# A routing softmax by silu in place of powers, with its planner's haste and logits changed, in a fused state-space and mixture-of-experts kernel

## The chip, the cores and the metric

The kernel runs on one core of a Trainium2 chip. A core has five engines that run side by side, each with its own queue in order: TensorE (PE, matrix products and transposes into PSUM), VectorE (DVE), ScalarE (ACT, activation functions from a loaded table), GpSimd (POOL), and SyncE (SP), which here only issues DMA transfers. They wait for one another through semaphores. The metric is the time of the program on the device in microseconds (us), the median of three runs.

## The reference

The input `x` is 16 sequences (blocks) of 512 positions with 128 features. Two layers follow one another, each with a residual: a linear state-space layer, then a layer of 8 experts of which all are computed and mixed by weights.

```python
x = x + layernorm(ssm(layernorm(x)))        # B_w, C_w, 64 rotating states, D
x = x + layernorm(ffn(layernorm(x)))

def ffn(x):                                  # E = 8 experts, F = 512
    router_probs = softmax(x @ w_router)             # 8 per position
    gate_weights = softmax(x @ w_gating / 0.1)       # 8 per position
    g = einsum("bsh,ehf->ebsf", x, w_gate)
    u = einsum("bsh,ehf->ebsf", x, w_up)
    expert_out = einsum("ebsf,efh->ebsh", silu(g) * u, w_down)
    cw = router_probs * gate_weights
    cw = cw / (sum(cw) + 1e-9)
    return einsum("ebsh,bse->bsh", expert_out, cw)
```

The part that the change touches is the routing: the two softmaxes and `cw`, 16 exponentials per position.

## The kernel before

**Work and slots.** A block is 512 positions. Its expert work is cut into 32 slots: 8 experts with 4 pieces of 128 hidden units. In slot n the kernel issues on TensorE the gate product `g` (`up`, three matmuls of 128x512), the up product `uu` (three), and, four slots late (`LAG`), the down product `d` of an earlier slot (`down`, three). Three matmuls stand for one product because every operand is split into a high part and a low rest (`mm3`, lines 354 to 357: high x high, low x high, high x low). ACT turns `g` into `sg` by silu (L601), DVE multiplies `sg` and `uu` (`gate`, L612), ACT makes the high part `hi` (L617), and the low rest `lo` (L623) is made on POOL or on DVE: `lo_pool[n]` picks POOL when the planner's sum for POOL is below that for DVE. If it is POOL, the product goes to an SBUF tile `hh`; otherwise it stays in the PSUM bank of `uu`, which is free only when DVE has made `lo`. There are two banks for `g`, three for `uu`, two for `d`, and a single one, tag "f", for all else.

**The planner.** The other work is written as generators: `front(b)` (the state-space layer of block b and the normalised input `xh`, `xl` of its experts), `route(b)` (the routing), `back(b)` (the last normalisation and the output). Each `yield` names how many slots later at the earliest the next step may come, its costs in us on DVE, ACT and POOL, and "f" where it takes the shared PSUM bank. `steps` (L834) goes through the open generators in each slot and issues a step if the planner's sums (`take`, a slot of 1.94 us) leave room for it. So the order on each engine's queue is fixed when the program is built. `begin` opens the chain of block b 67 slots before its experts (`LEAD`), block 1 at slot 0, block 2 at slot 4. A chain with `hurry` gets two steps a slot and loses one slot of each wait; block 1 has it, and blocks 2 and 3 get it 16 slots ahead of their experts. Steps of a hurried chain that take the bank are issued ahead of the slot's `g`.

**The routing.** The logits are 16 numbers a position. Blocks 0 to 2 get them from four full-precision matmuls of 16 columns (`lg`, L436); later blocks (`wide`, L264) from two matmuls of 512 columns (`lp`, L443 and L444) with four copies of the split router weights `wr4`, which DVE transposes in four pieces (`lt`, L450). DVE takes the maximum (L456) and subtracts it (L457). The exponentials: in block 0 two ACT instructions with `Exp` (L462, L463); in all other blocks eight POOL instructions that raise the constants e and e^10 (`bases`) to the power of the logits (L467). DVE then sums, inverts and scales (L470 to L472), multiplies the two softmaxes (L476), sums, adds 1e-9, inverts (L478 to L480), writes the result into a padded tile (`cwp`, L483) and transposes it (`cwT`, L485). Four DMAs on SP's queue write it to DRAM and further ones read it back, spread over all partitions (`cwb`, L502), for `combine`, which weighs each expert's output.

**The start.** Up to the first slot the state-space layer of block 0 runs by itself with all engines on one chain: rotation tables on DVE, `u` (normalised input, ACT L552), its transposes and `bu` on TensorE, a scan on DVE, `yp` on TensorE. ACT's queue begins with two DMA issues, the copies of bT and cT (L283, L284), two diagonals (L693, L694) and `u`. SP's queue issues the loads in the order in which the code names them; the router and gating weights (`wrg`, L136 and L137) come behind the first three expert weights. The first splits of expert weights are partly made on TensorE (`rest`), partly on POOL (`wgl`, `wul`, `wdl`, L117).

Of the kernel before, what the change touches and what calls it, by code (L numbers as in the profile page):

```python
# [2 lines left out]

# [8 lines left out]
F32 = mybir.dt.float32  # L12
F32R = mybir.dt.float32r
AF = mybir.ActivationFunctionType
ALU = mybir.AluOpType
# [8 lines left out]
N = 64  # L24
# [5 lines left out]
OWN = 8  # L30
WARM = 4
AHEAD = 3
FILL = 8
LN_EPS = 1e-5


# [12 lines left out]
def sandwich(ctx, tc, x, a_params, B_w, C_w, Dv, w_router, w_gating, w_gate, w_up, w_down, sines, out):  # L49
# [71 lines left out]
    small_ins = work("small_ins")  # L121
    st = small_ins[: N // 2, :P]
    nc.sync.dma_start(out=st, in_=sines)
    av = const.tile([N // 2, 1], F32, name="av")
    act.dma_start(out=av, in_=a_params.unsqueeze(1))
    load_x(0)
    bw = small_ins[:N, P : 2 * P]
# [7 lines left out]
    wrg = const.tile([D, 2, E], F32, name="wrg")  # L135
    nc.sync.dma_start(out=wrg[:, 0], in_=w_router)  # L136
    nc.sync.dma_start(out=wrg[:, 1], in_=w_gating)  # L137
    dbc = const.tile([P, D], F32, name="dbc")
    for k in range(AHEAD, OWN):
        load_w(k)  # L140
# [5 lines left out]
    make_identity(nc, ident)  # L146
    neghalf = const.tile([P, NT], F32, name="neghalf")
    gp.memset(neghalf, -0.5)
    zero = const.tile([P, 1], F32, name="zero")
    gp.memset(zero, 0.0)  # L150
    bases = const.tile([P, NT, 2, E], F32, name="bases")
    gp.memset(bases[:, :, 0], math.e)
    gp.memset(bases[:, :, 1], math.exp(10.0))
    cwp = []
    for i in range(2):
        t = const.tile([P, NT, 32], F32, name=f"cwp{i}")
# [105 lines left out]


    def wide(b):  # L264
        return b > 2

    bT = [const.tile([D, P], F32R, name=f"bT{i}") for i in range(2)]
    cT = const.tile([P, D], F32, name="cT")
# [1 line left out]
    bT32 = const.tile([D, P], F32, name="bT32", tag="first")  # L270

    wr4 = []

    const.tile([P, FILL], F32, name="fill")

    def transposed_weights():
        pb = bank(ps_u, "u", "pb")[:, :N]
# [76 lines left out]
    def mm3(ps, w, cs, mh, ml, first, last):  # L354
        pe.matmul(ps, w[0][:, cs], mh, start=first, stop=False)  # L355
        pe.matmul(ps, w[1][:, cs], mh, start=False, stop=False)  # L356
        pe.matmul(ps, w[0][:, cs], ml, start=False, stop=last)  # L357
# [67 lines left out]
    def route(b):  # L425

        G2 = NT * 2
        yield 1, 0, 0, 0, "f"
        bc = lambda t, n: t.unsqueeze(2).broadcast_to([P, n, E])
        ez = small.tile([P, G2, E], F32, name="ez", bufs=2)  # L430
        mx = small.tile([P, G2], F32, name="mx", bufs=2)
        if not wide(b):
            lg = ps_f.tile([P, G2, E], F32, name=f"lg{b}", tag="f")
            xT = blocks[b]["xT"]
            for c in range(NT):
                pe.matmul(  # L436
                    lg[:, 2 * c : 2 * c + 2], xT[:, P * c : P * c + P], wrg.rearrange("d g e -> d (g e)"),
                    start=True, stop=True,
                )
            yield 1, 0.4, 0, 0  # L440
        else:
            lp = ps_f.tile([P, T], F32, name=f"lp{b}", tag="f")
# [8 lines left out]
            own[0] = False  # L451
            yield 1, 0.7, 0, 0
            l4 = lt.rearrange("p j (i k) -> p j i k", i=2)
            vec.tensor_tensor(ez.rearrange("p (c g) e -> p c (g e)", g=2), l4[:, :, 0], l4[:, :, 1], ALU.add)
            lg = ez
        vec.tensor_reduce(mx, lg, AX.X, ALU.max)  # L456
        vec.tensor_tensor(ez, lg, bc(mx, G2), ALU.subtract)  # L457
        if not wide(b):
            own[0] = False
        if b == 0:  # L460
            e4 = ez.rearrange("p (c g) e -> p c g e", g=2)
            act.activation(e4[:, :, 0], e4[:, :, 0], AF.Exp)  # L462
            act.activation(e4[:, :, 1], e4[:, :, 1], AF.Exp, scale=10.0)  # L463
        else:
            for i in range(G2):
                yield 1, 0, 0, 1.62
                gp.tensor_tensor(ez[:, i], bases.rearrange("p c g e -> p (c g) e")[:, i], ez[:, i], ALU.pow)  # L467
        yield 2, 0.65, 0, 0
        sm = small.tile([P, G2], F32, name="sm", bufs=2)
        vec.tensor_reduce(sm, ez, AX.X, ALU.add)  # L470
        vec.reciprocal(sm, sm)
        vec.tensor_tensor(ez, ez, bc(sm, G2), ALU.mult)  # L472
        yield 1, 0.75, 0, 0
        pr = ez.rearrange("p (c g) e -> p c g e", g=2)
        cw0 = small.tile([P, NT, E], F32, name="cw0", bufs=2)
        vec.tensor_tensor(cw0, pr[:, :, 0], pr[:, :, 1], ALU.mult)  # L476
        cs = small.tile([P, NT], F32, name="cs", bufs=2)
        vec.tensor_reduce(cs, cw0, AX.X, ALU.add)  # L478
        vec.tensor_scalar(cs, cs, 1e-9, None, ALU.add)
        vec.reciprocal(cs, cs)  # L480
        yield max(1, 32 * b - 8 - now[0]), 0.45, 0, 0
        cwt = cwp[b % 2]
        vec.tensor_tensor(cwt[:, :, 0:E], cw0, bc(cs, NT), ALU.mult)  # L483
# [105 lines left out]
    dps = {}  # L589
    late = []  # L590

    def up(n):
        b, e, fc = n // 32, n // 4 % 8, n % 4
        B = blocks[b]
        cs = slice(128 * fc, 128 * fc + 128)
        g = ps_g.tile([P, T], F32, name=f"g{n}", tag="g")
        mm3(g, W[0, e], cs, B["xh"], B["xl"], True, True)
        u = ps_u.tile([P, T], F32, name=f"uu{n}", tag="u")
        mm3(u, W[1, e], cs, B["xh"], B["xl"], True, True)
        s = hp.tile([P, T], F32, name=f"sg{n}", tag="sg", bufs=2)  # L600
        act.activation(s, g, AF.Silu)  # L601
        pend[n] = s, u
# [49 lines left out]
    def chain(b):  # L652
        yield from front(b)
        yield from route(b)
# [147 lines left out]

    def first():
        nonlocal routed
        for _ in range(2):
            next(first_route)
        routed = next(first_route)

# [25 lines left out]
    def steps(n, ahead=False):  # L834

        for x in list(side):
            hurry = x[3]
            for _ in range(1 + hurry):
                bank = "f" in x[1][3:]
                if ahead != bool(hurry and bank):  # L840
                    break
                if n >= x[0] and not (own[0] and bank) and take(x[1][:3]):
                    own[0] = own[0] or bank
                    y = next(x[2], None)
                    if y is None:
                        side.remove(x)
                        break
                    x[0], x[1] = n + (y[0] if y[4:] else max(y[0] - hurry, 0)), y[1:]

    own[0] = False  # L850
    for n in range(total + LAG):
# [5 lines left out]
        if 0 <= n - 1 < total:  # L857
            take((0, 0, 1.23) if lo_pool[n - 1] else (0.6, 0, 0), (9, 9, 9))
            split_hi(n - 1)
        for step in side:  # L860
            if step[4] in (2, 3) and n == 32 * step[4] - 16:
                step[3] = 1
        if n < total:
            steps(n, True)
            if n == 0:
                first()
            up(n)
        if n == 0:
# [61 lines left out]
```

## Time and profile before

| | |
|---|---|
| median of 3 runs | 1125.45 us (1125.32 to 1125.46) |
| profiled execution | 1125.5 us, of it 1123.7 between the first and the last instruction |
| TensorE busy | 1105.3 us, 98% |
| DVE, POOL, ACT busy | 882.6, 781.3, 710.8 us |
| first expert matmul | 24.19 us |
| last 6.7 us | TensorE busy 0.54 us |
| powers on POOL | 120 instructions of 1.65 us, 195.9 us |
| table loads on ACT | two of 1.28 us, at 1.77 and 25.33 us |

"busy" is the time in which an engine has an instruction in work. Matmuls overlap, so the duration of one (0.39 us) is longer than the step from one to the next; how much work TensorE gets through is read from starting times. A name such as `L612` is a line of the kernel before. An answer of the timeline has the start and the duration in us, then engine, line, operation, output and inputs, shape and number; in brackets stands how long the engine was idle before it and what ended that. A row of a group ends with busy time, mean duration in ns, and idle time before.

### The profile page before, as it was taken

The numbers are of one execution on the slowest core, as the hardware profiler recorded it, in microseconds if no ns is written. First come the engines' busy times: TensorE is split into PE (matmuls) and PEld (weight loads), VectorE is DVE, ScalarE is ACT, GpSimd is POOL, SyncE is SP. The second block draws the span as 40 slices with busy tenths as digits, with TensorE's granted clock in tenths as the row PEclk, the third lists the DMA queues.
The fourth block names the chain that finished last, engine by engine and source line by source line (L and its number), as shares of the span: only waits on it lengthen the run. The fifth ranks groups of instructions, "written<-read, shape, count | busy, mean of one in ns | idle before, by whom it ended". The sixth has DMA issues, their size and how long they took to land.

```text
span 1123.7 us, 16035 instructions
## 1 busy us (share of the span) xinstructions
PE 1105.3 (98%) x4909; PEld 906.6 (81%) x4909; DVE 882.6 (79%) x2056; ACT 710.8 (63%) x1347; POOL 781.3 (70%) x651
## 2 busy tenths in 40 slices
PE   7999999999999999999999999999999999999997
PEld 5778888878878888888888888888888888888886
DVE  7887777887878888787887878878787887777666
ACT  4775756666565665766666675666766666666563
POOL 2688685786959568685876768668685876848452
PEclk9999999999999999999999999999999999999999
DMA  5240402212131221302203130130312202121020
GB/s 157 74 133 1 123 29 84 68 39 85 38 114 29 58 66 57 94 29 76 76 30 94 38 113 29 57 92 17 110 29 76 76 20 75 29 76 30 29 76 10
DMA packets 66950, 71.22 MB, mean 63 GB/s; under 512 B 7216, under 2 KB 49328, under 8 KB 66864
## 3 DMA queue, kind: packets, MB, share of 16 engines
q1 hardware_dynamic: 66448, 70.04, 20.8%
q8 instruction: 38, 0.62, 0.2%
q14 instruction: 48, 0.39, 0.1%
q10 hardware_dynamic: 416, 0.16, 0.1%
HBM read 54.98 MB, written 15.20 MB: 62 GB/s over the span
## 4 chain that ended last, share of the span: by engine, by line
PE 90%; DVE 4%; POOL 2%; ACT 1%; issue 1%; DMA 0%; DVEq 0%; POOLq 0%; ACTq 0%
PE g L355 10%; PE g L356 10%; PE g L357 10%; PE d L355 10%; PE d L357 10%; PE d L356 10%; PE uu L355 10%; PE uu L356 10%; PE uu L357 10%; PE yp L404 1%; POOL ez L467 1%; ACT sg L601 1%; DVE uu L612 0%; DVE lo L623 0%; DVE hh L612 0%
## 5 line engine op out<-in xcount | busy, mean ns | idle before, releaser
L617 ACT CAST hi<-uu 128x512 fp32r<-128x512 f32 x325 | 191.0, 588 | 219.8 <-DVE uu L612 205.6
L623 POOL TENSOR_TENSOR lo<-hh,hi 128x512 fp32r<-128x512 f32 x187 | 244.8, 1309 | 120.8 <-ACT hi L617 118.2
L601 ACT ACTIVATE sg<-g 128x512 f32<-128x512 f32 x512 | 306.8, 599 | 20.8 <-PE g L357 17.2
L612 DVE TENSOR_TENSOR uu<-sg,uu 128x512 f32<-128x512 f32 x325 | 225.1, 692 | 105.8 <-ACT sg L601 103.1
L623 DVE TENSOR_TENSOR lo<-uu,hi 128x512 fp32r<-128x512 f32 x325 | 223.0, 686 | 102.9 <-ACT hi L617 97.5
L646 POOL TENSOR_TENSOR acc<-acc,ct 128x512 f32<-128x512 f32 x109 | 147.3, 1351 | 94.9 <-DVE ct L643 90.2
L617 ACT CAST hi<-hh 128x512 fp32r<-128x512 f32 x187 | 116.2, 621 | 149.6 <-DVE hh L612 146.0
L355 PE MATMUL g<-xh,wgh 128*128 128x512 f32 x512 | 202.6, 396 | 0.8 <-ACT sg L601 0.4
L355 PE MATMUL uu<-xh,wuh 128*128 128x512 f32 x512 | 199.7, 390 | 2.6 <-DVE lo L623 2.4
L356 PE MATMUL g<-xh,wgl 128*128 128x512 f32 x512 | 199.5, 390 | 0.0
L357 PE MATMUL g<-xl,wgh 128*128 128x512 f32 x512 | 199.5, 390 | 0.0
L356 PE MATMUL uu<-xh,wul 128*128 128x512 f32 x512 | 199.3, 389 | 0.0
L357 PE MATMUL uu<-xl,wuh 128*128 128x512 f32 x512 | 199.3, 389 | 0.0
L355 PE MATMUL d<-hi,wdh 128*128 128x512 f32 x512 | 199.3, 389 | 0.0
L356 PE MATMUL d<-hi,wdl 128*128 128x512 f32 x512 | 199.2, 389 | 0.0
L357 PE MATMUL d<-lo,wdh 128*128 128x512 f32 x512 | 199.2, 389 | 0.0
L467 POOL TENSOR_TENSOR ez<-bases,ez 128x8 f32<-128x8 f32 x120 | 195.9, 1652 | 1.6 <-DVE ez L457 1.6
L612 DVE TENSOR_TENSOR hh<-sg,uu 128x512 f32<-128x512 f32 x187 | 127.1, 680 | 11.0 <-ACT sg L601 9.2
L355 PEld LDWEIGHTS g<-xh,wgh 128*128 128x128 f32 x512 | 96.2, 188 | 24.5 <-ACT sg L601 5.7
L355 PEld LDWEIGHTS uu<-xh,wuh 128*128 128x128 f32 x512 | 96.1, 188 | 24.4 <-DVE lo L623 4.3
L357 PEld LDWEIGHTS g<-xl,wgh 128*128 128x128 f32 x512 | 96.1, 188 | 20.3
L356 PEld LDWEIGHTS uu<-xh,wul 128*128 128x128 f32 x512 | 96.1, 188 | 20.2
(185 smaller groups left out, 1346.8 us busy)
## 6 DMA issues: line engine op xcount, KB each, us to landing
cwb<-scw SPq DMA_DIRECT2D x48, 512.0 KB
cwb<-scw SPq DMA_DIRECT2D x32, 256.0 KB
xt<-in_L_attn_u_dram SPq DMA_DIRECT2D x15, 256.0 KB
sco<-ob SPq DMA_DIRECT2D x60, 64.0 KB
ot<-sco SPq DMA_DIRECT2D x15, 256.0 KB
out_dram<-x SPq DMA_DIRECT2D x15, 256.0 KB
scr_u<-blk_u SPq DMA_DIRECT2D x52, 64.0 KB
ft_u<-scr_u SPq DMA_DIRECT2D x13, 256.0 KB
```

Source lines behind the costliest of these rows:

```text
L355: pe.matmul(ps, w[0][:, cs], mh, start=first, stop=False)
L356: pe.matmul(ps, w[1][:, cs], mh, start=False, stop=False)
L357: pe.matmul(ps, w[0][:, cs], ml, start=False, stop=last)
L404: pe.matmul(yp[:, c], v[:, P * c : P * c + P], cT, start=True, stop=True)
L467: gp.tensor_tensor(ez[:, i], bases.rearrange("p c g e -> p (c g) e")[:, i], ez[:, i], ALU.pow)
L601: act.activation(s, g, AF.Silu)
L612: vec.tensor_tensor(h, s, u, ALU.mult)
L617: act.copy(hi, pend[n])
L623: (gp if lo_pool[n] else vec).tensor_tensor(lo, h, hi.bitcast(F32), ALU.subtract)
L646: add = lambda: eng.tensor_tensor(acc, acc, t, ALU.add)
```

## The change

- The exponentials of all blocks come from ACT's silu. With y = logit - maximum and S = silu(y - 1), S / ((y - 1) - S) equals e^(y - 1), and the constant factor drops out of the softmax. So `route` gets one `Silu` instruction for all 64 columns with a bias of -1, and DVE gets a subtraction of both, a reciprocal of 64 columns and a product.
- The two softmaxes are no longer scaled one by one: `zz` is the product of the unscaled exponentials, one reduction sums the three parts, and the 1e-9 is scaled by the product of two sums.
- The powers and `bases` go, and `Exp` of block 0 goes.
- The factor 10 of the gating logits is put into the weights: ACT scales `wrg[:, 1]` right behind its two DMA issues.
- `wide` holds from block 1 on, and `wr4` is made in slot 16.
- Blocks 2 and 3 get no haste. Block 1's chain starts in slot 4 with haste, block 2's in slot 5. Bank steps of a hurried chain come between `g` and `uu`.
- `av` lies in `small_ins`; the tile `fill` goes.

```diff
-    av = const.tile([N // 2, 1], F32, name="av")
+    av = small_ins[: N // 2, T - 1 : T]
     nc.sync.dma_start(out=wrg[:, 1], in_=w_gating)
+
+    act.activation(wrg[:, 1], wrg[:, 1], AF.Copy, scale=10.0)
...
-    zero = const.tile([P, 1], F32, name="zero")
+    zo = const.tile([P, 2], F32, name="zo")
+    zero, minus1 = zo[:, 0:1], zo[:, 1:2]
     gp.memset(zero, 0.0)
-    bases = const.tile([P, NT, 2, E], F32, name="bases")
-    gp.memset(bases[:, :, 0], math.e)
-    gp.memset(bases[:, :, 1], math.exp(10.0))
+    gp.memset(minus1, -1.0)
...
     def wide(b):
-        return b > 2
+        return b > 0
...
         vec.tensor_reduce(mx, lg, AX.X, ALU.max)
-        vec.tensor_tensor(ez, lg, bc(mx, G2), ALU.subtract)
+        vec.tensor_tensor(y, lg, bc(mx, G2), ALU.subtract)
         if not wide(b):
             own[0] = False
-        if b == 0:
-            e4 = ez.rearrange("p (c g) e -> p c g e", g=2)
-            act.activation(e4[:, :, 0], e4[:, :, 0], AF.Exp)
-            act.activation(e4[:, :, 1], e4[:, :, 1], AF.Exp, scale=10.0)
-        else:
-            for i in range(G2):
-                yield 1, 0, 0, 1.62
-                gp.tensor_tensor(ez[:, i], bases.rearrange("p c g e -> p (c g) e")[:, i], ez[:, i], ALU.pow)
-        yield 2, 0.65, 0, 0
-        sm = small.tile([P, G2], F32, name="sm", bufs=2)
-        vec.tensor_reduce(sm, ez, AX.X, ALU.add)
-        vec.reciprocal(sm, sm)
-        vec.tensor_tensor(ez, ez, bc(sm, G2), ALU.mult)
-        yield 1, 0.75, 0, 0
-        pr = ez.rearrange("p (c g) e -> p c g e", g=2)
-        cw0 = small.tile([P, NT, E], F32, name="cw0", bufs=2)
-        vec.tensor_tensor(cw0, pr[:, :, 0], pr[:, :, 1], ALU.mult)
+        yield 1, 0, 0.25, 0
+        act.activation(ez, y, AF.Silu, bias=minus1)
+
+        own[0] = own[0] and not wide(b)
+        yield 1, 0.7, 0, 0
+        vec.scalar_tensor_tensor(y, y, 1.0, ez, ALU.subtract, ALU.subtract)
+        vec.reciprocal(y, y)
+        vec.tensor_tensor(ez, ez, y, ALU.mult)
+        yield 1, 0.95, 0, 0
+        vec.tensor_tensor(zz, e4[:, :, 0], e4[:, :, 1], ALU.mult)
+
+        sm = small.tile([P, G2 + NT], F32, name="sm", bufs=2)
+        vec.tensor_reduce(sm, zq, AX.X, ALU.add)
+        s2 = sm[:, :G2].rearrange("p (c g) -> p c g", g=2)
         cs = small.tile([P, NT], F32, name="cs", bufs=2)
-        vec.tensor_reduce(cs, cw0, AX.X, ALU.add)
-        vec.tensor_scalar(cs, cs, 1e-9, None, ALU.add)
+        vec.tensor_tensor(cs, s2[:, :, 0], s2[:, :, 1], ALU.mult)
+        vec.scalar_tensor_tensor(cs, cs, 1e-9, sm[:, G2:], ALU.mult, ALU.add)
         vec.reciprocal(cs, cs)
...
-    def up(n):
+    def up(n, between):
         mm3(g, W[0, e], cs, B["xh"], B["xl"], True, True)
+        between()
         u = ps_u.tile([P, T], F32, name=f"uu{n}", tag="u")
...
-        for step in side:
-            if step[4] in (2, 3) and n == 32 * step[4] - 16:
-                step[3] = 1
         if n < total:
-            steps(n, True)
             if n == 0:
                 first()
-            up(n)
+            up(n, lambda: steps(n, True))
         if n == 0:
             begin(n, 0, first_route, 1, routed)
-            if NB > 1:
-                begin(n, 1, chain(1), 1)
...
-        if n == 32:
+        if n == 16:
             w4 = wrg.rearrange("d g e -> d (g e)").unsqueeze(1).broadcast_to([D, 4, 2 * E])
...
         for i in range(NB):
-            if i > 1 and n == max(4, 32 * i - LEAD):
-                begin(n, i, chain(i))
+            if i > 0 and n == max(i + 3, 32 * i - LEAD):
+                begin(n, i, chain(i), i == 1)
```

`first`, which issues block 0's logits and the start of its routing ahead of slot 0, takes one step more, so that the silu is issued there.

More of the change, by code (lines that the diff above doesn't have):

```diff
@@ L1 @@
-import math
 from contextlib import ExitStack
@@ L32 @@
 AHEAD = 3
-FILL = 8
 LN_EPS = 1e-5
@@ L272, in sandwich @@
     wr4 = []
-    const.tile([P, FILL], F32, name="fill")
     def transposed_weights():
@@ L429, in route @@
         bc = lambda t, n: t.unsqueeze(2).broadcast_to([P, n, E])
-        ez = small.tile([P, G2, E], F32, name="ez", bufs=2)
+        y = small.tile([P, G2, E], F32, name="y", bufs=1)
+        zq = small.tile([P, G2 + NT, E], F32, name="zq", bufs=2)
+        ez, zz = zq[:, :G2], zq[:, G2:]
+        e4 = ez.rearrange("p (c g) e -> p c g e", g=2)
         mx = small.tile([P, G2], F32, name="mx", bufs=2)
@@ L450, in route @@
                 vec.transpose(lt[k].rearrange("p j i -> p (j i)"), lp[k, P * q : P * q + P])
-            own[0] = False
             yield 1, 0.7, 0, 0
             l4 = lt.rearrange("p j (i k) -> p j i k", i=2)
-            vec.tensor_tensor(ez.rearrange("p (c g) e -> p c (g e)", g=2), l4[:, :, 0], l4[:, :, 1], ALU.add)
-            lg = ez
+            vec.tensor_tensor(y.rearrange("p (c g) e -> p c (g e)", g=2), l4[:, :, 0], l4[:, :, 1], ALU.add)
+            lg = y
         vec.tensor_reduce(mx, lg, AX.X, ALU.max)
-        vec.tensor_tensor(ez, lg, bc(mx, G2), ALU.subtract)
+        vec.tensor_tensor(y, lg, bc(mx, G2), ALU.subtract)
@@ L482, in route @@
         cwt = cwp[b % 2]
-        vec.tensor_tensor(cwt[:, :, 0:E], cw0, bc(cs, NT), ALU.mult)
+        vec.tensor_tensor(cwt[:, :, 0:E], zz, bc(cs, NT), ALU.mult)
         cwT = small.tile([P, NT, 32], F32, name="cwT", tag="cwT", bufs=2)
@@ L804, in first @@
         nonlocal routed
-        for _ in range(2):
+        for _ in range(3):
             next(first_route)
```

## The prediction

> **What bounds the kernel now.** I read the page first: TensorE against the rest, and the chain that ended last.
>
> ```profile
> span 1123.7 us, 16035 instructions
> ...
> PE 1105.3 (98%) x4909; PEld 906.6 (81%) x4909; DVE 882.6 (79%) x2056; ACT 710.8 (63%) x1347; POOL 781.3 (70%) x651
> ...
> PE 90%; DVE 4%; POOL 2%; ACT 1%; issue 1%; DMA 0%; DVEq 0%; POOLq 0%; ACTq 0%
> ```
>
> TensorE is full. So relief elsewhere counts only where TensorE waits. Where that is, the busy time by stretches tells (columns: stretch, its length, then busy time of each engine):
>
> ```profile
> 24.20:36.40 12.20, 9.58 (x40) 6.33 (x39) 9.46 (x32) 7.67 (x17) 6.68 (x7) 1.00 0.01 2
> 36.40:99.70 63.30, 61.75 (x278) 49.14 (x279) 52.57 (x104) 46.27 (x91) 53.09 (x43) 1.00 0.30 92
> ...
> 205.00:355.00 150.00, 148.46 (x657) 120.90 (x656) 119.75 (x269) 92.94 (x181) 111.65 (x91) 1.00 0.22 65
> 355.00:1000.00 645.00, 645.00 (x2886) 534.71 (x2886) 514.57 (x1172) 417.64 (x785) 466.46 (x380) 1.00 0.20 60
> ```
>
> From 355 to 1000 us TensorE is busy 645.00 of 645.00 us, although the powers sit on POOL there too. Nothing can be won there by emptying POOL. Third, TensorE's timeline:
>
> ```profile
> 5.12 1.86 PE L178 MATMUL hot<-ident 128*128 128x96 f32 x8
> ...
> 12.77 0.58 PE L178 MATMUL hot<-ident 128*128 128x96 f32 x4
> 14.11 0.71 PE L739 MATMUL yp<-cT,spare 128*128 128x128 f32 x4 [0.76 <-DVE spare L738]
> ...
> 16.80 0.38 PE L739 MATMUL yp<-cT,spare 128*128 128x128 f32 x1 [0.26 <-DVE spare L738]
> ...
> 31.56 0.40 PE L357 MATMUL g<-xl,wgh 128*128 128x512 f32 x1
> 33.60 0.50 PE L355 MATMUL uu<-xh,wuh 128*128 128x512 f32 x1 [1.64 <-DVE lo L623]
> ...
> 600.91 0.39 PE L355 MATMUL g<-xh,wgh 128*128 128x512 f32 x1
> ...
> 602.95 0.39 PE L355 MATMUL g<-xh,wgh 128*128 128x512 f32 x1
> ```
>
> A steady slot takes 2.04 us (602.95 - 600.91), nine matmuls at 0.227; slots 0 to 3 have no `d` and need 1.36. In the same timeline a slot with `bu` takes 0.70 more, with two-pass logits `lp` 0.46, with `yp` 0.91 (the next slot's 0.10 included), with four-column logits `lg` 0.95 (0.14 included), with four transposes 0.36. Against these needs the first `g` of slots 0, 5, 32, 64, 96, 128, 160, 192 (24.19, 36.36, 99.72, 168.38, 236.01, 304.21, 373.99, 441.65) leaves as lost: 4.33 in slots 0-4, 3.75 in 5-31, 0.81, 0.27, 0.81, 2.39, 0.27 in blocks 1 to 5; later blocks take 67.39 each with nothing lost. So 12.6 us can be lost at most less, beside the start before 24.19.
>
> What makes the first loss, by the timelines of DVE and POOL:
>
> ```profile
> 30.21 0.91 DVE L472 TENSOR_TENSOR ez<-ez,sm 128x64 f32<-128x64 f32 x1
> 31.15 1.17 DVE L476 TENSOR_TENSOR cw<-ez 128x32 f32<-128x32 f32 x1
> ```
>
> ```profile
> 29.75 1.28 POOL L623 TENSOR_TENSOR lo<-hh,hi 128x512 fp32r<-128x512 f32 x1
> 30.99 1.28 POOL L117 TENSOR_TENSOR wdl<-raw,wdh 128x512 fp32r<-128x512 f32 x1
> ```
>
> These two take 0.23 and 0.18 elsewhere; here each ends when POOL's 128x512 instruction ends (31.03, 32.27). A DVE instruction with both inputs in SBUF waits for such a POOL instruction; against a power on POOL L472 kept its 0.23.
>
> **Part 1: the scaling of the gating weights at the head of ACT's queue.** It waits for `w_gating`.
>
> ```profile
> 5.16 0.43 SPq L137 DMA_DIRECT2D wrg<-in_L_ffn_w_gating_dram  x1
> ```
>
> ```profile
> 4.05 0.27 ACT L283 COPY bT<-pb 128x128 f32<-128x128 f32 x1 [1.00 <-PE pb L278]
> ...
> 6.55 0.49 ACT L552 ACTIVATE u<-xt,nmh,rsh 128x128 f32<-128x128 f32 x1 [0.42 <-DVE nmh L548]
> ```
>
> The semaphore of that load ends at 7.98 in this trace, behind three 256 KB weight loads. Everything behind it on ACT waits: the copies of bT and cT, the two diagonals, then `u` (6.55). At ACT's own pace from 8.05 (0.2, 0.17, 0.17, 0.21, 0.3 from start to start) `u` starts near 9.05: 2.5 late, and with it the transposes, `bu` and `yp` L713. TensorE's waits for DVE ahead of both L739 groups (0.76 and 0.26, some 0.3 more because modelled ends overlap) absorb about 1.3; 1.2 reaches the second L739, the statistics behind it and so the first `g`. Beyond that TensorE now idles some 2.6 us before the transposes, and it starts slow: eight `hot` in 1.86 (0.23 each) at 5, four in 0.58 (0.145) at 12.8. If the pace comes later by up to 3 us of such work, a further 3 x (1 - 0.145/0.23) = 1.1. Bounds: 0 (absorbed) to 2.6; I take +1.8.
>
> [...]
>
> **Part 2: slots 0-4.** Two exponentials (0.23, 0.21) go and one silu comes (128x64; bounds 0.23 for 128x32 and 0.49 for 128x128, I take 0.33). The built instruction order still has two table loads: one ahead of the scaling, one ahead of the first silu. The load (1.28, at 25.33) no longer stands behind DVE's subtraction but directly behind the weight cast that ends at 24.46, so the first `sg` comes 0.6 earlier. Then DVE, counted from the first `g`: `uu` 2.45-3.15; the new subtraction of both meets POOL's `wdl` (three weight parts now run back to back, 0.35 to 4.14) and ends at 4.37; reciprocal of 64 columns (L471 takes 0.204 for 8, L480 0.178 for 4: 0.0065 per column, so 0.57); product 0.23; `lo` to 5.78, `hh` to 6.43; five small ones to 7.43; the last product meets POOL's `lo` (to 8.43), the transpose, `uu` of slot 2 to 9.55, its cast 10.20, `sg` of slot 3 10.73, the `g` of slot 5 at 10.8. Before it stood at 12.17 with 0.36 of transposes that now come in slot 9: **-1.0**. Bounds: +1 if one more product meets POOL, -3 if none does.
>
> **Part 3: slots 5-31.** Block 1's front starts 4 slots later (8 us), so its statistics now meet slots 4-7: the single-input `ve` waits for a weight part as L299 did (1.03 against 0.17), and I count 1.4 lost in slots 7-9. Behind that, the sum of DVE's durations over what TensorE's slots last runs up to 2.0-3.4 us of arrears in slots 12-24, where before 3-4.6 stood; I take 1.5 lost there. 2.9 for 3.75: **-0.8**; bounds -2.5 and +1.5. Block 1's weights `cwT` now stand in slot 32, and the product that needs them in slot 41, 18 us later; the four writes, first reads and landing took 8.3 us (34.61 to 42.9), so SP's queue hides them. `xh` comes in slot 28 for slot 32.
>
> **Part 4: powers and haste gone.**
>
> ```profile
> L467 POOL TENSOR_TENSOR ez<-bases,ez 128x8 f32<-128x8 f32 x120 | 195.9, 1652 | 1.6 <-DVE ez L457 1.6
> ```
>
> POOL loses 196 us; by the built order its `lo` go from 187 to 239 (52 x 1.31 = +68), DVE's from 325 to 273 (-36 us). DVE's routing grows by some 0.5 us a block (reciprocal 0.57; `sm`, `cs` reductions and small ones about even), ACT's by 0.33, under its slack. The new wait: DVE's subtraction waits for the silu, which stands on ACT behind `sg` and two norms (2 x 0.39); DVE idles some 0.4, and the gate queued behind it needs the next `sg` anyway. Arrears in blocks 3-12 reach 1.7 us, before 3.1. The 3.47 lost in blocks 3-5 (among them `bu` waiting for the logits' transposes at 336, now three slots apart) should go to 0.5: **-3.0**, bounds -3.5 and 0. Blocks 1-2: about equal (1.08 to 1.0, **-0.1**).
>
> **Part 5: logits in two passes** for blocks 1 and 2, on TensorE itself: 2 x (0.95 - 0.46) = **-1.0**. The tail does not change; `av` inside `small_ins`, the constants, and bank steps of block 1 between `g` and `uu` issue the same instructions, nothing.
>
> Sum: +1.8 - 1.0 - 0.8 - 3.0 - 0.1 - 1.0 = -4.1 on the profiled 1125.5 (span 1123.7 and 1.8 around it; the median 1125.45 is the same): **1121.4 us**.
>
> **Rivals.**
> A, the forecast: own range 1118.5 to 1124.
> B, slower: POOL's freed time goes into 128x512 instructions, and DVE's six new two-input instructions in each block meet them. For: the 1.17 above; 52 more `lo`. Against: blocks 6-12 lose nothing today with larger arrears. A gate may come about 2.7 us late before `sg`'s bank stops TensorE (`g` two slots on, 4.08, less 0.85, 0.6); three waits of 1.2 pass that by 0.9. At half of it over 13 blocks: +5.9, 1127.3; it decides from 0.3 us a block.
> C, the start costs its bound of 2.6 and slots 0-31 give nothing: 1125.5 + 2.6 - 3.0 - 1.1 = 1124.0, to 1126 if slots 5-9 lose more than counted. For: both terms rest on races of tenths of a microsecond.
> D, the start is absorbed and nearly all of the losses go: 1125.5 - 9.0 = 1116.5.
> E, it does not do what it says: the second table load stays, as shown; that is counted in A.
>
> **How the numbers follow.** Chances: A 0.58, B 0.16, C 0.18, D 0.08. No change means within 0.2%, 2.25 us: 1123.2 to 1127.7. Faster: 0.50 of A and D, 0.58. Same: 0.08 of A, 0.16 of C, 0.02 of B, 0.26. Slower: 0.14 of B, 0.02 of C, 0.16. Range 1117.0 to 1127.2: it leaves out half of D and of B.
>
> **What would show it.** Right: `u` at about 9 us and the first `g` near 26; two table loads; slot 5 about 10.8 after slot 0; no wait of TensorE between 240 and 430; 67.39 per block after. Wrong: `u` still at 6.6 (part 1 falls), small DVE instructions of 1 us in every block with TensorE waits beside them (B), a slot pace other than 2.04 (none of this).

## The result, and the profile after

The changed kernel takes 1141.76 us (median of 4 runs, 1140.26 to 1142.95) against 1125.38 for the kernel before on the same chip (1125.29 to 1125.46): a ratio of 1.0144, 95% interval 1.0132 to 1.0156. It is slower by 16.4 us, where 1121.4 was forecast with a range up to 1127.2. The profiled execution took 1141.7 us, its span is 1139.9.

The page after, its busy times and the shares of the chain that ended last:

```profile
span 1139.9 us, 15980 instructions
...
PE 1117.7 (98%) x4897; PEld 900.8 (79%) x4897; DVE 901.2 (79%) x2030; ACT 701.3 (62%) x1362; POOL 653.2 (57%) x582
...
PE 71%; DVE 14%; issue 7%; ACT 4%; POOL 1%; DMA 0%; DVEq 0%; ACTq 0%; POOLq 0%
```

No engine is much busier than before, and POOL has lost 128 us. But TensorE's share of the chain has fallen from 90% to 71%, and DVE's has risen from 4% to 14%. The next view has the busy time by stretches of the kernel after, cut at the first `g` of slots 0, 5, 32, 192 and 416 (columns: stretch, its length, then the busy time of PE, its weight loads, DVE, ACT and POOL):

```profile
25.86:36.30 10.44, 8.59 (x35) 5.87 (x35) 7.71 (x20) 5.74 (x11) 5.08 (x4) 1.00 0.01 2
36.30:101.38 65.08, 62.40 (x275) 48.70 (x276) 55.20 (x116) 48.02 (x98) 50.58 (x45) 1.00 0.29 90
101.38:445.80 344.42, 343.31 (x1508) 277.53 (x1507) 279.95 (x623) 213.93 (x419) 206.26 (x182) 1.00 0.21 62
445.80:928.96 483.16, 481.33 (x2108) 388.00 (x2107) 391.72 (x848) 298.22 (x581) 278.75 (x246) 1.00 0.21 63
```

Against the same slots before (first `g` at 24.19, 36.36, 99.72, 441.65 and 913.40):

| stretch | before, us | after, us | difference |
|---|---|---|---|
| up to the first `g` | 24.19 | 25.86 | +1.67 |
| slots 0 to 4 | 12.17 | 10.44 | -1.73 |
| slots 5 to 31 | 63.36 | 65.08 | +1.72 |
| blocks 1 to 5 | 341.93 | 344.4 | +2.5 |
| blocks 6 to 12 | 471.75 | 483.2 | +11.4 |
| the rest of the span | 210.3 | 210.9 | +0.6 |

The sum is +16.2, the difference of the spans. Most of it lies where the forecast had put nothing: each of the blocks 6 to 12 takes 69.02 us in place of 67.39, with the same 2108 matmuls. Those seven blocks before the change:

```profile
441.65:913.38 471.73, 471.73 (x2108) 391.27 (x2107) 376.87 (x861) 306.74 (x576) 344.93 (x281) 1.00 0.21 63
```

The granted clock is 1.00 in all these stretches, so it is no slower TensorE.

The last row after the change has a trap. TensorE is "busy" for 481.33 of 483.16 us although it lost 11.4 us there: a matmul lasts 0.39 us but the next one starts 0.227 us after it, so a gap shorter than 0.16 us leaves no idle time, and a longer one shows only by its excess. The list of waits, asked for that stretch alone, is clearer (columns: us in total, times, longest):

```profile
ACT hi L617 <- DVE uu L612: 101.6, 98, 2.1
...
PEld g L352 <- ACT sg L601: 13.1, 28, 0.5
...
PEld uu L352 <- DVE lo L623: 3.1, 13, 0.3
```

`g` waits for `sg` to free its bank; the list has four such waits in each block. The starting times of the matmuls, which also show the short waits, have eight slots that are too long, the same in every block: 20 to 23 (1.0 us together), 27 and 28 (0.4), 3 and 4 (0.2).

What made DVE late is in its timeline, here slots 18 to 21 of block 8, and in POOL's for the same time:

```profile
622.93 1.04 DVE L459 TENSOR_TENSOR y<-y,mx 128x64 f32<-128x64 f32 x1
...
624.49 1.73 DVE L395 TENSOR_TENSOR_SCAN v<-v,zo 128x512 f32<-128x512 f32 x1
...
627.71 0.55 DVE L468 RECIPROCAL y<-y 128x64 f32<-128x64 f32 x1
628.30 1.20 DVE L469 TENSOR_TENSOR zq<-zq,y 128x64 f32<-128x64 f32 x1
...
630.02 0.71 DVE L471 TENSOR_TENSOR zq<-zq 128x32 f32<-128x32 f32 x1
```

```profile
622.60 1.30 POOL L646 TENSOR_TENSOR acc<-acc,ct 128x512 f32<-128x512 f32 x1 [0.70 <-DVE ct L643]
623.84 1.31 POOL L623 TENSOR_TENSOR lo<-hh,hi 128x512 fp32r<-128x512 f32 x1
...
628.13 1.29 POOL L623 TENSOR_TENSOR lo<-hh,hi 128x512 fp32r<-128x512 f32 x1 [0.54 <-ACT hi L617]
629.40 1.29 POOL L316 TENSOR_TENSOR x<-ot,x 128x512 f32<-128x512 f32 x1
```

The subtraction (shortest of its kind 0.22) ends when `acc` ends, the product of silu and reciprocal (0.22) when `lo` ends, the product of the softmaxes (0.19) when `x` ends, and the scan (1.21 alone) gets 0.5 longer beside `lo`. The reciprocal has one input and keeps its 0.55; here it meets a `lo` only in its last 0.13, but the one at 213.45 us stands wholly beside POOL's `v` (213.30 to 214.60) and also takes 0.55.

It is not only the new instructions. Two groups that the change does not touch, `ve` and `xl`, in the kernel before and in the one after, there with the new product of silu and reciprocal below them (columns at the end: busy time, mean ns, idle before):

```profile
L299 DVE TENSOR_SCALAR ve<-mv 128x4 f32<-128x4 f32 x60 | 21.7, 362 | 2.1
...
L422 DVE TENSOR_TENSOR xl<-ft_x,xh 128x512 fp32r<-128x512 f32 x15 | 12.6, 843 | 1.0 <-ACT xh L419 1.0
```

```profile
L296 DVE TENSOR_SCALAR ve<-mv 128x4 f32<-128x4 f32 x60 | 37.1, 618 | 2.1
...
L419 DVE TENSOR_TENSOR xl<-ft_x,xh 128x512 fp32r<-128x512 f32 x15 | 22.1, 1470 | 0.0
L469 DVE TENSOR_TENSOR zq<-zq,y 128x64 f32<-128x64 f32 x16 | 16.8, 1050 | 0.6
```

`ve` takes 15.4 us more. In a block of before, one of its four met a 128x512 instruction of POOL and one ran beside a power, which did not hold it up; this is block 8, first DVE's timeline, then POOL's:

```profile
628.10 0.17 DVE L299 TENSOR_SCALAR ve<-mv 128x4 f32<-128x4 f32 x1
```

```profile
626.32 3.24 POOL L467 TENSOR_TENSOR ez<-bases,ez 128x8 f32<-128x8 f32 x2
```

(POOL's row holds two powers, to 629.56.) In the changed kernel the `ve` of the same step comes while POOL's `acc` runs, and takes 1.14 (641.57). `xl` takes 9.5 us more, for another reason: no power ran beside it. In blocks 6 to 12 before, it started 0.42 us ahead of a `lo` of POOL; now it starts 0.17 behind an `acc` and waits. I sum for each group of ten or more DVE instructions what they last beyond the group's tenth percentile: 44.7 us before, 88.0 after. DVE's durations in all grew by 23.2 us although 52 low rests (0.69 each, 36 us) moved to POOL, so 59 us came on top, three quarters of them stretched instructions (a little more in truth, for in a group like `zq` L469 fifteen of sixteen are stretched, the tenth percentile with them).

### The profile page after: what moved, and what is told of

Its sections match the earlier page's. It is cut to its first block, busy times and chain, and to the rows that moved or that the text cites. A ratio compares the mean times of both kernels' runs of the same rounds, so it can differ in the third digit from the quotient of the medians.

```text
span 1139.9 us, 15980 instructions
## 1 busy us (share of the span) xinstructions
PE 1117.7 (98%) x4897; PEld 900.8 (79%) x4897; DVE 901.2 (79%) x2030; ACT 701.3 (62%) x1362; POOL 653.2 (57%) x582
## 4 chain that ended last, share of the span: by engine, by line
PE 71%; DVE 14%; issue 7%; ACT 4%; POOL 1%; DMA 0%; DVEq 0%; ACTq 0%; POOLq 0%
PE g L352 8%; PE g L354 8%; PE g L353 8%; PE uu L353 8%; PE uu L354 8%; PE uu L352 8%; PE d L354 7%; PE d L352 7%; PE d L353 7%; ACT sg L601 3%; DVE hh L612 3%; DVE uu L612 3%; DVE lo L623 2%; DVE ct L643 1%; DVE v L395 1%
## 5 line engine op out<-in xcount | busy, mean ns | idle before, releaser
L623 POOL TENSOR_TENSOR lo<-hh,hi 128x512 fp32r<-128x512 f32 x239 | 316.2, 1323 | 219.9 <-ACT hi L617 214.4
L612 DVE TENSOR_TENSOR uu<-sg,uu 128x512 f32<-128x512 f32 x273 | 188.5, 691 | 134.8 <-ACT sg L601 133.0
L617 ACT CAST hi<-uu 128x512 fp32r<-128x512 f32 x273 | 160.3, 587 | 213.9 <-DVE uu L612 201.9
L617 ACT CAST hi<-hh 128x512 fp32r<-128x512 f32 x239 | 148.5, 621 | 199.6 <-DVE hh L612 196.6
L623 DVE TENSOR_TENSOR lo<-uu,hi 128x512 fp32r<-128x512 f32 x273 | 187.0, 685 | 73.7 <-ACT hi L617 67.0
L646 POOL TENSOR_TENSOR acc<-acc,ct 128x512 f32<-128x512 f32 x109 | 142.5, 1307 | 159.7 <-DVE ct L643 113.1
L352 PE MATMUL g<-xh,wgh 128*128 128x512 f32 x512 | 207.1, 404 | 5.0 <-ACT sg L601 1.9
L612 DVE TENSOR_TENSOR hh<-sg,uu 128x512 f32<-128x512 f32 x239 | 161.9, 678 | 12.1 <-issue 9.3
L352 PEld LDWEIGHTS g<-xh,wgh 128*128 128x128 f32 x512 | 96.1, 188 | 44.7 <-ACT sg L601 27.4
L354 PEld LDWEIGHTS uu<-xl,wuh 128*128 128x128 f32 x512 | 96.1, 188 | 20.5
L352 PEld LDWEIGHTS d<-hi,wdh 128*128 128x128 f32 x512 | 96.1, 188 | 20.5
```

Source lines behind the costliest of these rows:

```text
L612: vec.tensor_tensor(h, s, u, ALU.mult)
L617: act.copy(hi, pend[n])
L623: (gp if lo_pool[n] else vec).tensor_tensor(lo, h, hi.bitcast(F32), ALU.subtract)
L646: add = lambda: eng.tensor_tensor(acc, acc, t, ALU.add)
```

## The experiments

In the texts on record, P is the theory that DVE's small instructions wait for POOL's 128x512 ones, R that the silu path's own work on DVE is too much, O (O2) that the order which the planner gives is the cause. V, W and L are told where they come up. The kernels named c_ and the late scaling have their lines behind 137 two lower than the kernel after where they are quoted. "A block" is the mean of blocks 6 to 12. Times without a range (runs 2, 3, 4, 8 and 10) are of one execution.

**1. The scaling moved behind the weight casts** (all the rest as changed).

```diff
-    act.activation(wrg[:, 1], wrg[:, 1], AF.Copy, scale=10.0)
...
         parts(k)
+    act.activation(wrg[:, 1], wrg[:, 1], AF.Copy, scale=10.0)
```

> The changed kernel with the scaling of the gating weights issued behind the five weight casts on ACT instead of at the head of its queue. If the wait for the gating weights made the start longer: u near 6.6 us, first g at 24.2 instead of 25.86, total about 1140.0 (1141.7 - 1.7). If the start was longer for another reason (constants moved, other table): first g stays near 25.9, total 1141.7.

1140.46 us (1140.17 to 1140.48; ratio 1.0132, 1.0115 to 1.0149). The first `g` comes at 24.12 in place of 25.86, 1.74 earlier, and the median falls by 1.3 (the intervals of the two ratios overlap, so the first `g` is the firmer sign). The wait for the weights costs about what it was said to; the main loss is untouched (69.05 us a block). Unless it is said otherwise, the kernels below start from this one.

**2. POOL's low rests left out** (from the kernel after).

```diff
+        if lo_pool[n]:
+            pend[n] = hi, hi
+            return
...
```

> The changed kernel with every low rest that POOL makes left out (the high part stands in for it in the down product), so TensorE, DVE and ACT issue the same instructions and only POOL's 239 big ones go. Theory P (DVE's small two-input instructions wait for POOL's big ones): a steady block falls from 69.0 to 67.4-67.7 us, total about 1124. Theory R (DVE's own added work, the reciprocal above all, is too much): stays at 69, total 1141. Theory O (the new order on the queues, ACT's norms and the silu ahead of hi): stays at 69 as well.

1120.5 us (P said about 1124), 67.48 a block. Taking away POOL's 239 low rests takes away the whole loss, with all of DVE's work still there. R falls as the whole cause. But P, too, holds only in part: DVE's stretching only fell from 88.0 to 73.5 us. `ve` still lasted 569 ns in the mean; what got short again were the product of silu and reciprocal (225 ns) and the scan (1240). So most of the stretched instructions cost nothing here; the loss went with these, which stand in slots 19 and 20.

**3. Powers again for blocks 3 to 15** in the new routing.

```diff
+        if b > 2:
...
+            for i in range(G2):
+                yield 1, 0, 0, 1.62
+                gp.tensor_tensor(ez[:, i], base, y[:, i], ALU.pow)
+        else:
...
+            act.activation(ez, y, AF.Silu, bias=minus1)
```

> The changed kernel (scaling late) with POOL's powers back for blocks 3 to 15 in place of silu, subtraction, reciprocal and product; the rest of the new routing and the plan stay. POOL's low rests fall from 239 to 186. Theories P and R: a steady block takes 67.4, total about 1122. Theory O2 (the plan without haste, shifted steps): stays above 68.5, total over 1137.

1138.9 us, 68.86 a block: P and R miss, and the number lies where O2 had it. DVE's stretching is back to 53 us, POOL's low rests to 186, and the waits in slots 3, 4, 27 and 28 are gone. But in every block `yp` now waits some 0.9 us in slot 22 for POOL's product L397, which stands behind a power and `x`, and the scan, two slots later than before, still meets a low rest (1749 ns in the mean). The edit moved the plan, so it did not undo one thing alone.

**4. The kernel before with the new routing** (silu, `zz`, one sum; old beginnings, haste and logits; the scaling late).

```diff
-                gp.tensor_tensor(ez[:, i], bases.rearrange("p c g e -> p (c g) e")[:, i], ez[:, i], ALU.pow)
...
+        act.activation(ez, y, AF.Silu, bias=minus1)
...
+        vec.scalar_tensor_tensor(y, y, 1.0, ez, ALU.subtract, ALU.subtract)
+        vec.reciprocal(y, y)
+        vec.tensor_tensor(ez, ez, y, ALU.mult)
```

> The kernel before with the new routing by silu alone (scaling late), old begin, haste and logits. POOL's low rests rise from 187 to 239. Theories P and R: a steady block takes about 69, total 1140 to 1144. Theory O2 (plan): 67.4, total about 1125.

1141.1 us, 69.02 a block. The routing alone brings the whole loss of the steady blocks, with the old haste and logits: O2 falls.

**5 to 7. Single collisions taken away.** Theory V: the stretched instructions nearest to a TensorE wait cause it, one by one. Theory W: DVE as a whole is short of time. Run 5 moves `ve` to POOL, run 6 the two products, run 7 both.

```diff
-        vec.tensor_scalar(ve, mv[:, :, 1], LN_EPS, None, ALU.add)
+        gp.tensor_scalar(ve, mv[:, :, 1], LN_EPS, None, ALU.add)
```

```diff
-        vec.tensor_tensor(ez, ez, y, ALU.mult)
+        gp.tensor_tensor(ez, ez, y, ALU.mult)
+        gp.tensor_tensor(zz, e4[:, :, 0], e4[:, :, 1], ALU.mult)
         yield 1, 0.95, 0, 0
-        vec.tensor_tensor(zz, e4[:, :, 0], e4[:, :, 1], ALU.mult)
```

> Against a_scale_late (1140.5 us) one thing is moved: the 128x4 addition `ve` of each normalisation is made by POOL, ahead of its own power `rs`, and no longer by DVE; nothing else changes its place. Theory V (a DVE instruction that can't run beside POOL's 128x512 ones; `ve` takes 1.1 us in place of 0.17 and holds up the gate products behind it): the TensorE waits at slots 3, 4, 27 and 28 of a steady block (0.07 + 0.11 + 0.26 + 0.11 = 0.55 us) go, 0.55 x 13 = 7 us: 1133 to 1135. Theory W (the block is short of DVE time as a whole, so a wait that is taken away comes back one slot on): 69.0 us a block stays, 1138 to 1141.

> Against a_scale_late (1140.5 us) the product of silu and reciprocal (128x64) and the product of the two softmaxes (128x32) are made by POOL, at the place where DVE made the first; order and plan are otherwise kept. Theory V: DVE no longer has a 1.2 us and a 0.7 us instruction in slots 20 and 21, the TensorE waits in slots 20 to 23 (0.37 + 0.11 + 0.33 + 0.11 = 0.92 us a block) go for the most part, 0.6 to 0.9 us x 13: 1129 to 1133; those in slots 3, 4, 27 and 28 stay. Theory W: 1138 to 1141.

> Both moves together. Theory V: 67.4 to 67.8 us a block as before the change; with the faster start of slots 0 to 5 (1.7 us) and no lost time in blocks 3 to 5 the time is 1119 to 1124, below the 1125.4 of before. Theory W: 1135 to 1141, and the waits appear in other slots.

1138.01 (1137.81 to 1138.11), 1139.83 (1139.67 to 1139.92) and 1138.38 us (1138.36 to 1138.68); ratios 1.0113 (1.0098 to 1.0128), 1.0129 (1.0114 to 1.0145) and 1.0117 (1.0100 to 1.0134). V fell: 2.4, 0.6 and 2.1 us came back of 7, 8 to 12 and 17 to 21. All three times lie where W had them. The wait moves to the next instruction that can be held up. In run 5's groups that is `ng`, which took 160 ns after the change:

```profile
L296 DVE TENSOR_SCALAR ng<-mv 128x4 f32<-128x4 f32 x60 | 35.5, 592 | 2.1
```

and in run 6's timeline, `cs` (0.21 and 0.16 after the change), beside POOL instructions of the same time:

```profile
626.36 0.72 DVE L475 TENSOR_TENSOR cs<-sm 128x4 f32<-128x4 f32 x1
627.11 1.20 DVE L476 SCALAR_TENSOR_TENSOR cs<-cs,sm 128x4 f32<-128x4 f32 x1
```

```profile
625.77 1.29 POOL L395 TENSOR_TENSOR v<-v,tre 128x512 f32<-128x512 f32 x1
627.02 1.28 POOL L621 TENSOR_TENSOR lo<-hh,hi 128x512 fp32r<-128x512 f32 x1
```

So these three runs tell that moving one instruction did not take the collisions away. That W's numbers came out does not show yet that DVE is short of time: runs 9 and 11 decide it.

**8. Empty steps in place of the powers.** The planner keeps their slots and their charge on POOL, POOL does nothing in them.

```diff
+        for i in range(G2 if b > 2 else 0):
+            yield 1, 0, 0, 1.62
```

> a_scale_late with the eight planner steps of the powers put back for blocks 3 to 15, each charged 1.62 us on POOL, but with no instruction in them: POOL gets about 50 low rests fewer (187 to 190 in place of 239) and DVE as many more, and POOL is idle where the powers were. Silu, reciprocal and products stay on DVE. Theory V in the form that the planner's answer is the cause (POOL's freed time is filled with 128x512 instructions, and DVE's small two-input instructions meet them): 67.4 to 67.9 us a block, 1121 to 1127. Rival (the DVE work of the silu path is too much in itself, wherever POOL's instructions fall): 68.6 us a block or more, 1135 or later.

1128.2 us, 1.2 above V's range; the mean block, 67.73, lies inside V's, and the rival's 1135 is far. POOL got 199 low rests. Blocks 2, 7, 10, 11 and 12 take 67.41 or 67.42 us; others take up to 68.9. With the silu work on DVE a block can lose nothing: R falls in its plain form too. The empty steps also put the rest of the routing some ten slots back (reciprocal and product of block 8 come in slots 30 and 31 in place of 20), so here, as in run 3, more than one thing moved.

**What was seen then.** Something must turn a late DVE into a late TensorE far more strongly than DVE's spare time (it is busy 391.72 of 483.16 us) suggests. From the timelines of block 8 I took how long after the first `g` matmul of a slot its `sg` ended (us):

```text
slot                     0     4     8    12    16    18    20    21    24    28
before                1.91  2.38  1.94  1.54  1.54  1.80  1.94  1.64  1.54  1.54
after                 3.63  3.87  3.21  2.78  2.62  3.73  5.18  5.34  3.56  3.87
2: no low rest on POOL 3.64 3.87  3.21  2.67  1.55  2.55  2.65  3.65  2.30  2.78
9: sg first           1.54  1.54  1.54  1.54  1.55  1.54  2.54  2.47  1.54  1.79
11: both orders       1.54  1.54  1.54  1.54  1.55  1.54  1.57  1.54  1.54  1.54
```

1.54 is as early as `g` allows. After the change `sg` is never on time, and a delay is worked off by only 0.14 us a slot (3.87 in slot 4, 2.78 in slot 12). Why, the timelines of DVE and then of ACT show, in the time of slots 4 and 5 of block 8 after the change (the work in them is that of slots 2 to 4):

```profile
592.19 0.69 DVE L612 TENSOR_TENSOR uu<-sg,uu 128x512 f32<-128x512 f32 x1
593.53 0.69 DVE L623 TENSOR_TENSOR lo<-uu,hi 128x512 fp32r<-128x512 f32 x1 [0.65 <-ACT hi L617]
594.14 0.68 DVE L612 TENSOR_TENSOR hh<-sg,uu 128x512 f32<-128x512 f32 x1
...
596.00 0.70 DVE L612 TENSOR_TENSOR uu<-sg,uu 128x512 f32<-128x512 f32 x1 [0.50 <-ACT sg L601]
```

```profile
592.91 0.59 ACT L617 CAST hi<-uu 128x512 fp32r<-128x512 f32 x1
593.39 0.60 ACT L601 ACTIVATE sg<-g 128x512 f32<-128x512 f32 x1
...
594.85 0.62 ACT L617 CAST hi<-hh 128x512 fp32r<-128x512 f32 x1
595.38 0.59 ACT L601 ACTIVATE sg<-g 128x512 f32<-128x512 f32 x1
```

There are two closed loops. ACT's queue has `hi` of a slot ahead of `sg` of the next one: product (594.14), `hi` (594.85), `sg` (595.38), next product (596.00), 1.86 us round. DVE's queue has `lo` of a slot ahead of the product of the next: product (592.19), `hi` (592.91), `lo` (593.53), next product (594.14), 1.95 us round. A slot is 2.04. Neither engine is full (DVE is busy for 81% of blocks 6 to 12, ACT for 62%), but whoever is late stays late for eight slots and more, and the next delay is added on top. When `sg` ends more than 4.08 us after its `g` (2.54 late), the `g` two slots on has no bank: the first such slot of block 8 is slot 2 (4.11), and slot 3 is the first that TensorE lengthens. That is theory L.

**9 to 12. The loops opened.** Run 9 gives ACT `sg` of slot n ahead of `hi` of slot n - 1, run 10 gives DVE the product of slot n ahead of `lo` of slot n - 1, run 11 both. Run 12 is the kernel before the change with both. No work is added or left out.

```diff
-            split_hi(n - 1)
         if n < total:
...
             up(n, lambda: steps(n, True))
+        if 0 <= n - 1 < total:
+            split_hi(n - 1)
```

```diff
-        if 0 <= n - 1 < total:
-            split_lo(n - 1)
         if n < total:
             lo_pool[n] = busy[2] < busy[0] and n < total - 3
             gate(n)
+        if 0 <= n - 1 < total:
+            split_lo(n - 1)
```

> Against a_scale_late (1140.5 us, 69.0 us a block) one thing is moved: ACT gets the silu `sg` of slot n ahead of the high part `hi` of slot n - 1; before, it came behind. No work is added or taken away. Theory L (a late DVE instruction is paid for many slots: product -> `hi` -> `sg` of the next slot -> next product is a closed loop of 1.85 to 1.95 us in a slot of 2.04, so that a delay of 1 us takes some 8 slots to work off, and the delays of a block add up until the banks of `g` run out): the loop over `sg` is open, TensorE's waits for `sg` go for the most part while DVE's instructions stay as stretched as they are (87 us over their shortest): 67.4 to 68.2 us a block, 1121 to 1130. Theory W (DVE has too little time in a block, whatever the order): 68.7 us or more a block, 1137 to 1141. The loop over DVE's own low rests (product -> `hi` -> `lo` -> next product) stays closed, so a part may remain.

> Against a_scale_late one thing is moved: DVE gets the product of slot n ahead of the low rest `lo` of slot n - 1. Theory L: this opens the other loop (product -> `hi` -> `lo` on DVE -> next product), which holds in about half of the slots; the loop over `sg` stays: 68 to 69 us a block, 1125 to 1139. Theory W: 69.0 us, 1138 to 1141.

> Both orders changed together. Theory L: no closed loop is left, 67.4 to 67.6 us in blocks 4 to 13, and with what the change gained in slots 0 to 5 (1.7 us): 1118 to 1122, faster than the 1125.4 of before. Theory W: 1136 to 1141.

> The kernel before with the same two orders changed. It lost nothing in its steady blocks, so only its 5.4 us in slots 0 to 31 behind the start and in blocks 1 to 5 can shrink. Theory L: 1119 to 1124. Theory W: 1125 to 1128 (nothing to gain, and `hi` comes later in each slot).

| run | us | ratio to before (95%) | a block, us | DVE's stretching, us |
|---|---|---|---|---|
| 9, `sg` first | 1120.58 (1120.47 to 1120.62) | 0.9956 (0.9940 to 0.9973) | 67.43 | 99.6 |
| 10, product first | 1126.3 | | 67.80 | 74.9 |
| 11, both | 1115.99 (1115.94 to 1116.18) | 0.9916 (0.9901 to 0.9931) | 67.41 | 93.5 |
| 12, before, both | 1121.45 (1121.15 to 1121.52) | 0.9964 (0.9951 to 0.9977) | 67.39 | 59.5 |

L holds and W falls. Runs 9 and 11 even came out 0.4 and 2 us below its range, for block 0 gains as well (75.41 us in run 1, 73.74 and 70.29 here). With one order changed and DVE's instructions stretched even more (99.6 us), the blocks lose nothing. Run 10 misses L's 68 to 69 us a block on the low side: with the loop over `sg` still closed, opening DVE's loop alone took away three quarters of the loss, more than L had said (the stretching fell with it, to 74.9). One wait is left there, `uu` for a low rest in slot 28, 0.39 us a block. Run 11 beats both kernels. Its stretch of slots 192 to 415, its ACT timeline there and its longest wait show a TensorE that never stops, an ACT whose `sg` starts on its own with `hi` behind it, and an ACT that now waits for TensorE (in the kernel after, this list has no such wait):

```profile
431.75:903.62 471.87, 471.87 (x2108) 391.21 (x2107) 389.69 (x848) 298.14 (x581) 277.43 (x246) 1.00 0.22 64
```

```profile
592.00 0.60 ACT L599 ACTIVATE sg<-g 128x512 f32<-128x512 f32 x1 [0.96 <-PE g L352]
592.50 0.58 ACT L615 CAST hi<-uu 128x512 fp32r<-128x512 f32 x1
...
594.04 0.60 ACT L599 ACTIVATE sg<-g 128x512 f32<-128x512 f32 x1 [0.44 <-PE g L352]
594.54 0.61 ACT L615 CAST hi<-hh 128x512 fp32r<-128x512 f32 x1
```

```profile
ACT sg L599 <- PE g L352: 156.0, 203, 1.6
```

Runs 11 and 12 also give the change its price with the loops open: 1115.99 against 1121.45, 5.5 us faster. Not all of that is work saved. In run 12's trace TensorE idles 2.8 us in slot 4 and then gets half the clock (0.50) in the 3.30 us of this stretch:

```profile
35.20:38.50 3.30, 3.30 (x11) 2.78 (x10) 1.42 (x6) 1.79 (x4) 2.28 (x2) 0.50 0.04 5
```

Slot 5 lasts 3.36 us there, against 2.15 in the kernel before, so some 1.2 us of the 5.5 are this. Run 11 has the scaling late, which was worth 1.3 (run 1). With the change as it stands, an estimated 4.2 are left, or 3.0 without the half-clock stretch of run 12.

## Why the prediction was wrong, step by step

**The step that failed** is in part 4: "Arrears in blocks 3-12 reach 1.7 us, before 3.1", so that blocks 6 to 12 were given no loss at all, and rival B's "against", that "blocks 6-12 lose nothing today with larger arrears". The delay of `sg` beyond its 1.54, the nearest to these arrears that the traces have, went the other way: in block 8 it reached 1.0 us before the change (slot 3) and 3.8 after it (slot 21). Two errors lie in the step. The first is the arrears' size. I counted the new DVE instructions at their undisturbed durations and let only them collide, and only in rival B, at 0.45 us a block. In the trace one `ve` of each block had run beside a power, and `xl` ahead of a `lo`; now both stand behind an `acc`, and with the new products' waits DVE lost 43 us more, 2.7 a block. The second is how fast arrears go. I took DVE's durations against TensorE's slots, which makes some 0.4 us a slot (DVE is busy four fifths of the time). The loops give back 0.14. Run 2 shows the first error's part (without POOL's low rests 67.48 us a block), runs 9 and 11 the second's (67.43 and 67.41 with the collisions in place).

**Rival B** was the right mechanism with 0.16 for its chance, and the sign that it named, small DVE instructions of 1 us in every block with waits of TensorE beside them, is what the trace shows. Its limit was right as well: it said that a product may come 2.7 us late; TensorE stopped when `sg` came 2.54 late. Its price of 0.45 us a block measured 1.63, and of the new two-input instructions only the two products are stretched by more than 0.2 us in most blocks. What it lacked was the loop, by which four delays of 0.5 to 1.0 us in slots 18 to 21 add to what is left over from the slots before, instead of starting from nothing.

**Part 1** held. +1.8 was said, +1.67 measured at the first `g`, and run 1 takes 1.74 back. (Run 2 has the same start, and its first `g` comes at 25.36, +1.17: some 0.5 us vary from one execution to another.) `u` started at 9.60 us where 9.05 was said, for the weights came later than in the trace of before:

```profile
8.68 0.21 ACT L137 ACTIVATE wrg<-wrg 128x8 f32<-128x8 f32 x1 [5.63 <-DMA wrg<-in_L_ffn_w_gating_dram]
...
9.60 0.49 ACT L551 ACTIVATE u<-xt,nmh,rsh 128x128 f32<-128x128 f32 x1
```

More of the 3.05 us by which `u` came later was absorbed than I had counted. The step from one small matmul (`yp`) to the next falls from 0.21 to 0.11 us near 15.6 us, before the change at 12.2: the faster pace came 3.4 later, and all the same the first `g` only 1.67 later. The forecast's "up to 3 us" for this was an assumption of mine, and no run shows what sets the moment.

**Part 2** held, number and way: slot 5 starts 10.44 us after slot 0 (10.8 said); counted from the first `g`, the subtraction that meets `wdl` ends at 4.23 (4.37 said) and the last product, which meets `lo`, at 8.33 (8.43). **Part 3** failed: slots 5 to 31 take 1.7 us more than before, where 0.8 less was said. With the loops open run 11 does them in 61.69 us in place of 65.08, so the step is in large part the same, arrears that were thought to go faster. But it is not the whole: run 12, the kernel before with open loops, takes 61.22, its half-clock stretch included. So the gain of 0.8 is not there without the loops either; where part 3 miscounted besides was not looked into.

**Parts 4 and 5** were to bring 4.1 us in blocks 1 to 5; these took 2.5 more. With the loops open on both sides (runs 12 and 11) they take 340.19 and 337.16 us, 3.0 less, so most of that gain exists, and the loops took it. I did not part haste, powers and logits from one another.

**Rival E**: the second table load is there, as was said (1.28 us at 26.16, the first at 1.77). Rivals C and D did not come.

What stays open: how much of DVE's delay in the closed loops is due to the collisions and how much to the new reciprocal and products. Measured as above, a block's stretching (mean of blocks 6 to 12) is 2.4 us before the change and 6.4 after. The good blocks of run 8 have 3.2 and lose nothing, so with half of the collisions the new work cost nothing; run 2 has 5.5 and loses 0.1, so it also matters where the collisions stand. No run has all collisions and none of the new work.

## What to carry to other kernels

A queue in order that has the second half of one piece of work ahead of the first half of the next ties two engines into a loop; compare the loop's time round with the slot, not the engines' busy shares, for the difference of the two is all that a delay is paid back with (here 1.86 and 1.95 us round against 2.04, and 0.14 paid back a slot). Where the kernel loses nothing, look at how late its producers are against their earliest time (here `sg` against `g`) before work is moved onto them. And when work is taken off an engine, ask what ran undisturbed beside it: its place is filled by whatever the planner puts there.

## What the runs showed of the hardware

- DVE's instructions with two inputs in SBUF, and also the single-input TENSOR_SCALAR of 128x4 (`ve`, and `ng` in run 5), waited in these traces until a running POOL instruction of 128x512 ended (`ve`: 1.14 in place of 0.17 us). In the kernel after, 31 `ve`, 15 products of silu and reciprocal (up to 1.31 in place of 0.22) and 12 `xl` (up to 1.68 in place of 0.68) began beside one that had over 0.1 us longer to run than they take, and all of them were held so. The reciprocal, with one input, was not (0.55 in all 16, two of them wholly beside one), nor was the product of `sg` and `uu`, whose `uu` lies in PSUM (0.65 to 0.70 in all 512). The wait goes the other way too. In the kernel before, DVE's scan starts first, and POOL's `acc`, 1.29 us elsewhere, takes 2.14:

```profile
612.62 1.22 DVE L398 TENSOR_TENSOR_SCAN v<-v,zero 128x512 f32<-128x512 f32 x1
```

```profile
612.78 2.14 POOL L646 TENSOR_TENSOR acc<-acc,ct 128x512 f32<-128x512 f32 x1 [1.07 <-DVE ct L643]
```

  There is an exception, in one direction: POOL's powers of 128x8 did not hold up `ve`, which kept 0.17 us in all 15 cases in which it started beside one before the change, nor the one scan that did so (1.22 us at 151.34). The other way the wait is there: the power that came up behind a running scan (at 414.26 before the change) took 2.56 us in place of 1.64.
- The same gaps of TensorE came in the same slots of every block (3, 4, 20 to 23, 27 and 28). The banks stayed as they were, and changing the order on ACT's and DVE's queues removed the gaps (69.05 us a block in run 1, 67.41 in run 11).
